# RWKV layer with routed experts: k and v of two token blocks as seven products in place of eight

## Chip, cores, metric

One core of one Trainium2 chip. The metric is device microseconds of one execution: 390.06 us for the kernel before (median of 3 runs, 389.13 to 390.11). Lower is better.

## The reference

An input x of 2048 tokens by 512 channels is layer-normed to xn. Two branches read xn, and their sum is added to x.

- *Attention branch.* `rvk = xn @ W_rvk.T` gives r, v and k. Over the tokens of a sequence runs a recurrence per channel (state o, q, p): `no2 = max(w + o, k)`, `A2 = exp(w + o - no2)`, `B2 = exp(k - no2)`, `q = A2 q + B2`, `p = A2 p + B2 v`, and its output is a quotient of two such sums. The result, times sigmoid(r), goes through `W_out`.
- *Expert branch.* A classifier gives 12 probabilities per token; the top 2 are taken. Eight of the 12 are experts (gate and up 512 to 256, silu, down 256 to 512), four pass xn through with a weight.

All is float32.

## The kernel before

Tokens are cut into four blocks of 512 (`NTB`), channels into four chunks of 128 (`CC`). A *unit* is one (block, chunk).

**Stages.** First each block is loaded, normed (`norm`, L196: VectorE statistics and scaling, ScalarE half of the scaling), transposed on TensorE (`turn_block`, L226, into `xnT`) and put through the classifier. Then routing (L377 to L553), a chain of small VectorE operations with a few matmuls, sorts the tokens into 25 tiles of 128, one expert each. `fill(n)` puts n projection matmuls between those stages, so that TensorE has work: 11 in the loop over blocks, 9, 15 and 7 in the routing, 14 while the first unit of the recurrence starts; 56 of 192.

**Projection** (`project`, L263). A unit takes 12 matmuls: for k, v and r four each, one per 128 input channels, added up in a PSUM bank. The profile shows each matmul as two MATMUL instructions. ScalarE takes the banks to SBUF: copies for k and v (L282), `exp(-r)` for r (L280).

**Recurrence** (`scan`, L286) has four stages per unit, emitted at separate points. First: VectorE copies the state column (L297), scans the running maximum (L301) and forms two exponents (L303, L304). Second: ScalarE's two exponentials (L306, L307). Third: two more scans and the products around them (L313 to L322). Fourth: GpSimd copies part of the last column to the state (L325) for the same chunk's next block, ScalarE the rest; VectorE takes a reciprocal (L327) and writes the product yT (L328). Units run block by block, (0,0), (0,1), ... (3,3), so that a state is next wanted four units later.

**Experts.** `first_half(i)` and `second_half(i)` per tile: GpSimd gathers rows (L561), the DMA transposes 16-bit halves with ScalarE copies around it, `up` (L613) is 4 matmuls, `activate` (L623) is tanh on ScalarE and two VectorE operations, `finish` (L657) is 2 matmuls, a weighting on ScalarE and a GpSimd scatter that adds into `out` (L665). Weights come through SP's queue, `fetch` (L569, 1 MB) and `fetch_down` (L582, 512 KB), each with three buffers.

**Output projection** (`attention`, L727): per 128 tokens 4 matmuls of yT with W_out, a VectorE operation, and for blocks 0 to 2 a GpSimd DMA that adds the rows into `out` (L753). Block 3 reads `out` back, adds and stores.

**Order.** Every engine runs its queue in the order in which the program emits it (`manual_schedule`). The main stretch is written out in a table (L783 to L816): each step has a planned time on TensorE's clock, the steps are sorted by it and emitted. Scan stages come every 19.0 us at offsets 0, 4, 6 and 12 from a start 7 us early; projection and the first two blocks' output projection are spread evenly; expert halves come every `spread`. After the table: output projection of block 2, a branch for surplus tiles that is not taken with these inputs' 25, and block 3.

Of the kernel before, what the change touches and what calls it, by code (L numbers as in the profile page):

```python
# [26 lines left out]
F32 = mybir.dt.float32  # L27
# [8 lines left out]
P = 128  # L36
# [23 lines left out]
def layer(ctx: ExitStack, tc: tile.TileContext, x, w_rvk, w_out, decay, first, cls, ebias, gu, down, out):  # L60
# [6 lines left out]
    keep = pool("keep", 1)  # L67
    xyp = pool("xy", 5)
    ewp = pool("ew", 3)
    gathered = pool("gathered", 2)  # L70
    wk1 = pool("wk1", 1)
    rows = pool("rows", 3)
    basep = pool("base", 4)
    rp = pool("route", 1)
    small = pool("small", 2)
    kvp = pool("kv", 5)
    erp = pool("er", 4)
    wk = pool("wk", 2)
# [12 lines left out]
    def load_x(b):  # L91

        if b < 3:
            t = ewp.tile([P, NJ, C], F32, tag="gw", name=f"x{b}")
        else:
            t = xyp.tile([P, NJ, C], F32, tag="xy", name=f"x{b}")
        for j in range(NJ):
            i = b * NJ + j
            nc.sync.dma_start(t[:, j, :], x[i * P : (i + 1) * P, :])
            xt[i] = t[:, j, :]  # L100
# [57 lines left out]
    for n in range(ET):  # L158
        nc.gpsimd.memset(rank[:, n : n + 1], float(ET - n))

    def iota(shape, pattern, cm, tag, dt, base=0):
        i32 = rp.tile([P, *shape], I32, tag=f"{tag}_i", name=f"{tag}_i")
        nc.gpsimd.iota(i32, pattern=pattern, base=base, channel_multiplier=cm)
        t = const.tile([P, *shape], dt, tag=tag, name=tag)
        nc.gpsimd.tensor_copy(t, i32)
        return t
# [6 lines left out]
    tok_p = iota([1], [[0, 1]], 1, "tok_p", F32)  # L173
    spare = iota([2], [[0, 2]], 1, "spare", F32, T + P)
    one8 = rp.tile([P, E], F32, tag="one8", name="one8")
    nc.gpsimd.memset(one8, 1.0)
# [49 lines left out]
    def turn_block(b):  # L226
        xnT[b] = xyp.tile([P, CC, TB], F32, tag="xy", name=f"xnT{b}")
        for c in range(CC):
            if c % 2 == 0:
                pt = ps_tr.tile([P, TB], F32, tag="tr", name=f"pt{b}_{c}")  # L230
            else:
                pt = ps_gu.tile([P, TB], F32, tag="gu", name=f"pt{b}_{c}")
            for j in range(NJ):
                nc.tensor.transpose(pt[:, j * P : (j + 1) * P], xt[b * NJ + j][:, c * P : (c + 1) * P], ident)
            nc.scalar.copy(xnT[b][:, c, :], pt)
# [26 lines left out]

    def project(b, c):  # L263

        n = f"{b}_{c}"
        for name, m in (("k", 2), ("v", 1), ("r", 0)):
            ps = ps_mm.tile([P, TB], F32, tag="mm", name=f"p{name}{n}")
            for k in range(CC):
                nc.tensor.matmul(  # L269
                    ps,  # L270
                    wrvk_sb[m][:, k, c * P : (c + 1) * P],
                    xnT[b][:, k, :],
                    start=(k == 0),
                    stop=(k == CC - 1),
                )
                if k < CC - 1:
                    yield
            t = (erp if name == "r" else kvp).tile([P, TB], F32, tag=name, name=f"{name}{n}")
            if name == "r":
                nc.scalar.activation(t, ps, AF.Exp, scale=-1.0)  # L280
            else:
                nc.scalar.copy(t, ps)  # L282
            kvr[b, c, name] = t
            yield

    def scan(b, c):  # L286

        n = f"{b}_{c}"
        s = state[c]
        w, cf = wdec[:, c : c + 1], cfac[:, c : c + 1]  # L290
        k = kvr[b, c, "k"]
        if c == 0:
            yT[b] = xyp.tile([P, CC, TB], F32, tag="xy", name=f"yT{b}")


        obv = wk.tile([P, 3, TB + 1], F32, tag="obv", name=f"obv{n}")
        nc.vector.tensor_copy(obv[:, :, 0:1], s[:, 0:3].unsqueeze(2))  # L297
# [10 lines left out]
        yield  # L308

        v = kvr[b, c, "v"]  # L310
        sums = wk1.tile([P, 2, TB], F32, tag="sums", name=f"sums{n}")
# [15 lines left out]
        nc.vector.reciprocal(den, den)  # L327
        nc.vector.tensor_mul(yT[b][:, c, :], num, den)  # L328
        yield

    units = [(b, c) for b in range(NTB) for c in range(CC)]
    LEAD = 4

    def whole(gen):
        for _ in gen:
            pass

    def all_products():
        for u in range(len(units)):
            yield from project(*units[u])  # L340

    products = all_products()

    def fill(n):
        for _ in range(n):
            next(products, None)

# [5 lines left out]
    for b in range(NTB):  # L353
        if b + 1 < NTB:
            norm(b + 1)
        fill(1 if b else 2)
        logits(b)
        fill(1 if b else 3)
        if b + 1 < NTB:
            turn_block(b + 1)  # L360
        add_quarters(b)


    def wide(tag, n=1):
        shape = [P, NT, ET] if n == 1 else [P, n, NT, ET]
        return rp.tile(shape, F32, tag=tag, name=tag)

# [56 lines left out]

    hot8 = rp.tile([P, 2, NT, E], F32, tag="hot8", name="hot8")
    nc.vector.tensor_copy(hot8, hot[:, :, :, :E])
# [18 lines left out]

    over = rp.tile([P, E, NT], F32, tag="over", name="over")
    nc.vector.tensor_tensor(
# [14 lines left out]
    nc.vector.tensor_tensor(pos, pc[:, :NT, :], per_tile(base, E), ALU.add)  # L462
    picked = rp.tile([P, 2, NT, E], F32, tag="picked", name="picked")
    nc.vector.tensor_tensor(
# [15 lines left out]
    def place_tiles():  # L480

        later = rp.tile([P, MAX_TILES, E - 1], F32, tag="later", name="later")
        nc.vector.tensor_tensor(
# [13 lines left out]
    NK = 2 * NT  # L497
    lowhot = xyp.tile([P, NK, P], BF16, tag="xy", name="lowhot")
    pi = ps_o.tile([P, NV, MAX_TILES], F32, tag="o", name="pi")
    fill(15)  # L500
    for m in range(2):
# [6 lines left out]
        )  # L508
        hh = rp.tile([P, NT, MAX_TILES], BF16, tag="hh", name=f"hh{m}")
        nc.vector.tensor_tensor(  # L510
# [4 lines left out]
        )  # L515
        tok = ewp.tile([P, NT, NV, MAX_TILES], BF16, tag="gw", name=f"tok{m}")
        nc.vector.tensor_tensor(
# [20 lines left out]
    nc.vector.tensor_scalar_mul(zw, zw, SCALE)  # L538
    pis = rp.tile([P, NV, MAX_TILES], F32, tag="pis", name="pis")
    nc.vector.tensor_copy(pis, pi)  # L540
# [28 lines left out]
    def fetch(i, which=which_i):  # L569
# [7 lines left out]
        )  # L577
        w = ewp.tile([P, CC, 2 * INTER], F32, tag="gw", name=f"gw{i}")
        nc.sync.dma_start(w, gu[bass.ds(e, 1)].rearrange("o p c n -> p (o c) n"))
        st[i].update(w=w, e=e)  # L580

    def fetch_down(i):  # L582
        d = ewp.tile([P, IC, C], F32, tag="dw", name=f"dw{i}")
        nc.sync.dma_start(d, down[bass.ds(st[i]["e"], 1)].rearrange("o p c n -> p (o c) n"))
        st[i]["d"] = d
# [88 lines left out]
    def first_half(i, n):  # L674

        if i + 2 < n:
            fetch(i + 2)
        if 0 < i < n - 1:
            flip_act(i - 1)
        up(i, (0, 1))  # L680
        if i == n - 1:
            turn_act(i - 1)
        up(i, (2, 3))
        activate(i)
        if i > 1:
            unite_act(i - 2)
        if i + 3 < n:
            gather(i + 3)

    def second_half(i, n):  # L690
# [5 lines left out]
        if i > 1:  # L696
            finish(i - 2)
        if i == n - 1:
            finish(i - 1)
        if 2 <= i + 1 < n:  # L700
            fetch_down(i + 1)

    xrows, orows = {}, {}

    def read_xn(b, js=range(NJ)):
        if b >= NTB - 2:
            t = ewp.tile([P, NJ, C], F32, tag="gw", name=f"xrows{b}")
        for j in js:
# [7 lines left out]
    def read_out(b):  # L716

        t = xyp.tile([P, NJ, C], F32, tag="xy", name=f"orows{b}")
        for j in range(NJ):
# [7 lines left out]
    def attention(b, js=range(NJ)):  # L727

        for j in js:
            i = b * NJ + j  # L730
            if i < (NTB - 2) * NJ - 2:
                po = ps_tr.tile([P, C], F32, tag="tr", name=f"pw{i}")
            elif j >= 2 if i in orows else j % 2 == 1:
                po = ps_mm.tile([P, C], F32, tag="mm", name=f"pw{i}")
# [23 lines left out]
    for i in range(2):  # L758
        fetch(i)
        fetch_down(i)  # L760
    fill(2)
    stages = [scan(*u) for u in units]
    next(stages[0])
    fill(3)
    next(stages[0])
# [10 lines left out]

    UNIT = 19.0
    after = {12: (0, 0), 13: (0, 1), 18: (0, 2), 19: (0, 3), 32: (1, 0), 33: (1, 1), 40: (1, 2), 41: (1, 3)}  # L780
    groups = 3 * (len(units) - LEAD) - 2 + len(after)
    total = groups * 3.43 + TILES * 5.2
    table = []  # L783
# [4 lines left out]
    for u in range(1, len(units)):  # L788
        for at in (0, 4, 6, 12):
            plan((u - 1) * UNIT - 7 + at, stages[u])  # L790
    one = total / groups / CC
    for m in range(groups):
        if m in after:
            b, j = after[m]
            group = attention(b, [j])
            plan(CC * m * one - 16, read_xn, b, [j])

            plan(CC * (m + 2 - j % 2) * one + 1, group)
        else:
            group = products  # L800
        for k in range(CC):
            plan((CC * m + k) * one, group)

# [85 lines left out]
```

## Time and profile before

| | |
|---|---|
| median of 3 runs | 390.06 us |
| profiled execution, its time | 389.55 us |
| its span, first to last instruction | 387.7 us |
| granted TensorE clock, mean | 0.999 |
| pk, pv, pr matmuls (L269) | 3 x 128 instructions, 60.0, 60.9, 60.2 us |
| expert matmuls (L619, L660) | 200 and 100 instructions, 90.1 and 47.1 us |
| output projection (L738) | 128 instructions, 57.5 us |
| reciprocals (L327, VectorE) | 16 x 3.346 us |
| GpSimd scatters (L665) | 25 x 1.661 us |

How to read it: PE is TensorE, DVE VectorE, ACT ScalarE, POOL GpSimd, SP the queue that starts most DMAs; L12 is line 12 of the kernel. A timeline row is start, length, engine, line, operation, output<-inputs, and in brackets the idle time before it and what ended that. The page's cost of a matmul row (595 ns) is longer than the distance from one to the next, because matmuls overlap in the pipeline. TensorE's last work is the output projection of block 3, from 374.0 to 383.7 us.

### The profile page before, as it was taken

To read this page: it belongs to the slowest core of one execution; us is meant where nothing else is said; L and a number is where in the kernel's file an instruction comes from. 1 tells how busy PE (TensorE), PEld (TensorE's weight loads), DVE (VectorE), ACT (ScalarE), POOL (GpSimd) and SP (SyncE) were. 2 spreads that over 40 slices of the span, in tenths; PEclk is the share of its full clock that TensorE was granted. 3 is DMA by queue.
4 is the path that set the end of the run, shared out by engine and by line. 5 is a ranking of instruction groups with operands and counts; after the bars stand their busy time and mean duration, and the time that the engine had idled before them with its cause. 6 is when DMAs were issued, how large, how long until landed. Compare 5 with 4: busy or idle time off the path is not lost. (4 is left out here: it accounts for less than half of the span.)

```text
span 387.7 us, 3521 instructions
## 1 busy us (share of the span) xinstructions
PE 372.0 (96%) x994; PEld 169.7 (44%) x994; DVE 270.6 (70%) x397; ACT 169.8 (44%) x278; POOL 94.4 (24%) x130
## 2 busy tenths in 40 slices
PE   0999999999999999999999999999999999999995
PEld 0465445544444444444444444444444444434442
DVE  5852899799969585858593948685866692949324
ACT  2566211344655554535653554645655354431000
POOL 5000300322232231334222243321322141113400
PEclk9999999999999999999999999999999999999999
DMA  7996945572799797999999897989899999673793
GB/s 285 394 378 251 325 137 193 191 210 63 158 265 304 182 329 194 252 262 230 328 264 266 162 269 213 288 231 230 210 292 274 266 188 236 166 219 46 91 201 115
DMA packets 62884, 88.80 MB, mean 229 GB/s; under 512 B 42192, under 2 KB 42320, under 8 KB 59088
## 3 DMA queue, kind: packets, MB, share of 16 engines
q1 hardware_dynamic: 55328, 67.85, 59.2%
q0 software_dynamic: 7536, 20.71, 24.4%
q8 instruction: 8, 0.13, 0.1%
q14 instruction: 12, 0.10, 0.1%
HBM read 63.78 MB, written 19.40 MB: 215 GB/s over the span
## 5 line engine op out<-in xcount | busy, mean ns | idle before, releaser
L619 PE MATMUL pg<-gw,xgT 128*128 128x512 f32 x200 | 90.1, 592 | 0.0
L665 POOL DMA_INDIRECT out_dram<-yo,to_i x25 | 41.5, 1661 | 156.1 <-ACT yo L664 88.1
L269 PE MATMUL pv<-xnT,wrvk 128*128 128x512 f32 x128 | 60.9, 595 | 1.1 <-DMA wrvk<-in_w_rvk_dram 1.1
L269 PE MATMUL pr<-xnT,wrvk 128*128 128x512 f32 x128 | 60.2, 596 | 0.0
L269 PE MATMUL pk<-xnT,wrvk 128*128 128x512 f32 x128 | 60.0, 600 | 0.0
L619 PEld LDWEIGHTS pg<-gw,xgT 128*128 128x128 f32 x200 | 37.8, 190 | 47.5 <-issue 45.9
L738 PE MATMUL pw<-wout_sb,yT 128*128 128x512 f32 x128 | 57.5, 593 | 0.1
L327 DVE RECIPROCAL den<-den 128x512 f32<-128x512 f32 x16 | 53.5, 3346 | 0.0
L628 DVE SCALAR_TENSOR_TENSOR th<-th,pg 128x256 f32<-128x256 f32 x25 | 10.5, 419 | 56.3 <-ACT th L627 56.3
L660 PE MATMUL po<-dw,actT 128*128 128x512 f32 x100 | 47.1, 593 | 0.8 <-ACT yo L664 0.8
L269 PEld LDWEIGHTS pk<-xnT,wrvk 128*128 128x128 f32 x128 | 24.5, 193 | 31.1 <-issue 30.3
L738 PEld LDWEIGHTS pw<-wout_sb,yT 128*128 128x128 f32 x128 | 24.2, 190 | 30.6 <-issue 30.6
L269 PEld LDWEIGHTS pv<-xnT,wrvk 128*128 128x128 f32 x128 | 23.9, 190 | 31.0 <-issue 28.6
L269 PEld LDWEIGHTS pr<-xnT,wrvk 128*128 128x128 f32 x128 | 23.8, 190 | 29.6 <-issue 28.9
L627 ACT ACTIVATE th<-pg 128x256 f32<-128x256 f32 x25 | 9.6, 383 | 60.4 <-PE pg L619 60.4
L561 POOL DMA_INDIRECT xg<-xs,token_i x25 | 26.1, 1046 | 37.9 <-DVE empty L548 27.4
L313 DVE TENSOR_TENSOR_SCAN sums<-obv,state,a 128x512 f32<-128x512 f32 x16 | 20.5, 1282 | 17.3 <-ACT obv L307 17.3
L660 PEld LDWEIGHTS po<-dw,actT 128*128 128x128 f32 x100 | 18.9, 190 | 25.1 <-issue 22.2
L607 ACT COPY xgT<-xq 128x1024 uint16<-128x1024 uint16 x25 | 29.0, 1160 | 0.0
L599 ACT COPY xp<-xg 128x1024 uint16<-128x1024 uint16 x25 | 26.2, 1046 | 3.5 <-DMA xq<-xp 3.5
L664 ACT ACTIVATE yo<-po,wplace 128x512 f32<-128x512 f32 x25 | 17.2, 687 | 22.3 <-PE po L660 22.3
L315 DVE TENSOR_TENSOR_SCAN sums<-obv,state,a 128x512 f32<-128x512 f32 x16 | 20.6, 1286 | 0.6
(153 smaller groups left out, 353.0 us busy)
## 6 DMA issues: line engine op xcount, KB each, us to landing
gw<-in_gu_dram SPq DMA_DIRECT2D x25, 1024.0 KB, 6.3
dw<-in_down_dram SPq DMA_DIRECT2D x25, 512.0 KB, 4.5
x<-in_x_dram SPq DMA_DIRECT2D x16, 256.0 KB, 6.0
xs<-x SPq DMA_DIRECT2D x16, 256.0 KB, 4.6
wrvk<-in_w_rvk_dram SPq DMA_DIRECT2D x3, 1024.0 KB
xrow<-xs SPq DMA_DIRECT2D x8, 256.0 KB, 4.4
out_dram<-xrow POOLq DMA_DIRECT2D x8, 256.0 KB, 4.0
xrows<-xs SPq DMA_DIRECT2D x8, 256.0 KB, 6.7
```

Of the source, the lines that this page charges most:

```text
L269: nc.tensor.matmul(ps, wrvk_sb[m][:, k, c * P : (c + 1) * P], xnT[b][:, k, :], start=(k == 0), stop=(k == CC - 1),)
L313: nc.vector.tensor_tensor_scan(sq, bs, a2, s[:, 3:4], ALU.add, ALU.mult)
L315: nc.vector.tensor_tensor_scan(sp, bvs, a2, s[:, 4:5], ALU.add, ALU.mult)
L327: nc.vector.reciprocal(den, den)
L561: nc.gpsimd.indirect_dma_start(out=xg, out_offset=None, in_=xs, in_offset=bass.IndirectOffsetOnAxis(ap=token[:, i : i + 1], axis=0),)
L599: nc.scalar.copy(xp, st[i]["xg"].bitcast(U16).rearrange("p (c h) -> p h c", h=2))
L607: nc.scalar.copy(xgT.bitcast(U16).rearrange("p c (t h) -> p c t h", h=2), st[i]["xq"].rearrange("p (h c) t -> p c t h", h=2),)
L619: nc.tensor.matmul(pg, st[i]["xgT"][:, c, :], st[i]["w"][:, c, :], start=(c == 0), stop=(c == CC - 1))
L660: nc.tensor.matmul(po, st[i]["actT"][:, c, :], st[i]["d"][:, c, :], start=(c == 0), stop=(c == IC - 1))
L664: nc.scalar.activation(yo, po, AF.Identity, scale=weight[:, i : i + 1])
L665: nc.gpsimd.indirect_dma_start(out=out, out_offset=bass.IndirectOffsetOnAxis(ap=to[:, i : i + 1], axis=0), in_=yo, in_offset=None, compute ...
L738: nc.tensor.matmul(po, yT[b][:, c, j * P : (j + 1) * P], wout_sb[:, c, :], start=(c == 0), stop=(c == CC - 1),)
```

## The change

Write the stacked weights of k and v as a 2 x 2 matrix of blocks A (rows: k, v; columns: input channels 0 to 255, 256 to 511), and xnT of two token blocks b, b+1 as B (rows: the same channel halves; columns: b, b+1). A B holds k and v of both blocks. Strassen's scheme in Winograd's form needs seven products:

p1 = A11 B11, p2 = A12 B21, p3 = S4 B22, p4 = A22 T4, p5 = S1 T1, p6 = S2 T2, p7 = S3 T3, with S1 = A21 + A22, S2 = S1 - A11, S4 = A12 - S2, S3 = A11 - A21, T1 = B12 - B11, T2 = B22 - T1, T3 = B22 - B12, T4 = B21 - T2. Then k(b) = p1 + p2, k(b+1) = p1 + p6 + p5 + p3, v(b+1) = p1 + p6 + p7 + p5, v(b) = p1 + p6 + p7 + p4.

```diff
+    def sum_weights():
+        nc.gpsimd.tensor_add(s1, a21, a22)
+        nc.gpsimd.tensor_sub(s2, s1, a11)
+        nc.gpsimd.tensor_sub(s4, a12, s2)
+        nc.gpsimd.tensor_sub(s3, a11, a21)          # s3 takes a21's place
+    def sum_x(b, part):
...
+        if part == 0:
+            nc.gpsimd.tensor_sub(t[:, 0], b12, b11)
+            nc.gpsimd.tensor_sub(t[:, 1], b22, t[:, 0])
+        else:
+            nc.gpsimd.tensor_sub(t[:, 0], b22, b12)
+            nc.gpsimd.tensor_sub(t[:, 1], b21, ts[b, 0][:, 1])
...
+    def p1(b, c):
+        ps = bank(ps_mm, "mm", f"px{b}_{c}")
+        yield from two(ps, a11, xnT[b][:, 0:2], c, True)
+        nc.scalar.copy(kvr_tile("v", b, c), ps)
+    def p2(b, c):
+        ps = banks[f"px{b}_{c}"]
+        yield from two(ps, a12, xnT[b][:, 2:4], c, False)
+        nc.scalar.copy(kvr_tile("k", b, c), ps)
+    def p6(b, c):
+        ps = bank(ps_tr, "tr", f"py{b}_{c}")
+        yield from two(ps, s2, ts[b, 0][:, 1], c, True)
+        if (b, c) == (0, 0):
+            yield
+        nc.vector.tensor_add(kvr_tile("k", b + 1, c), kvr[b, c, "v"], ps)
+    def p7(b, c):
+        ps = banks[f"py{b}_{c}"]
+        yield from two(ps, s3, ts[b, 1][:, 0], c, False)
+        nc.vector.tensor_add(kvr_tile("v", b + 1, c), kvr[b, c, "v"], ps)
+    def p5(b, c):
+        ps = bank(ps_mm, "mm", f"pz{b}_{c}") if (b, c) < (0, 2) else bank(ps_tr, "tr", f"pz{b}_{c}")
+        yield from two(ps, s1, ts[b, 0][:, 0], c, True)
+        nc.vector.tensor_add(v, v, ps)              # v(b+1)
+        if (b, c) == (0, CC - 1):
+            sum_x(2, 0)
+            sum_x(2, 1)
+    def p4(b, c):
+        ps = banks[f"py{b}_{c}"]
+        yield from two(ps, a22, ts[b, 1][:, 1], c, False)
+        nc.vector.tensor_add(v, v, ps)              # v(b)
+    def p3(b, c):
+        ps = banks[f"pz{b}_{c}"]
+        yield from two(ps, s4, xnT[b + 1][:, 2:4], c, False)
+        nc.vector.tensor_add(k, k, ps)              # k(b+1)
```

`two` is two matmuls, one per 128 input channels; r keeps its four, in two halves `r(b, c, h)`. The order of the products, cut to its form:

```diff
+        for c in (0, 2):
+            for part in (p1, p2):
+                yield from part(0, c)
+                yield from part(0, c + 1)
+        for c in range(3):
+            for b in (0, 1):
+                yield from r(b, c, 0)
+                yield from r(b, c, 1)
+        for part, c in (
+            (p6, 0), (p6, 1), (p7, 0), (p7, 1), (p4, 0), (p5, 0), (p4, 1), (p3, 0),
+            (p5, 1), (p6, 2), (r, 0), (p3, 1), (p6, 3), (r, 0), (p7, 2), (p7, 3),
+            (p4, 2), (p4, 3), (r, 1), (p5, 2), (r, 1), (p5, 3), (p3, 2),
+        ):
...
+        for c in range(CC):          # second pair: p1 r p6 r p2 p7 r p5 p4 r p3
```

The units run as (0,0), (1,0), (0,1), (1,1), ...: the other block of the same chunk follows at once. The sums of x and of the weights for the first pair are emitted on GpSimd in the loop over blocks, behind `turn_block(1)`. The other lines that bear on time:

```diff
-        obv = wk.tile([P, 3, TB + 1], F32, tag="obv", name=f"obv{n}")
+        obv = wk1.tile([P, 3, TB + 1], F32, tag="obv", name=f"obv{n}")
...
-        nc.vector.tensor_mul(yT[b][:, c, :], num, den)
+        nc.gpsimd.tensor_mul(yT[b][:, c, :], num, den)
...
-        w = ewp.tile([P, CC, 2 * INTER], F32, tag="gw", name=f"gw{i}")
+        w = place.tile([P, CC, 2 * INTER], F32, tag=f"s{7 - i % 2}", name=f"gw{i}")
...
-        if i + 2 < n:
-            fetch(i + 2)
         if 0 < i < n - 1:
             flip_act(i - 1)
         up(i, (0, 1))
...
         activate(i)
+        if i + 2 < n:
+            fetch(i + 2)
...
-    fill(2)
     stages = [scan(*u) for u in units]
     next(stages[0])
-    fill(3)
+    fill(5)
```

Behind these stand: ten shared 1 MB places s0 to s9 (blocks of x, xnT, the sums T, gate weights, yT, rows read back) in place of two pools; gate weights and down weights two buffers each for three; `fetch_down` behind `finish`; a smaller scratch for GpSimd's DMA descriptors (4096). In the table there are 176 products for 192 and 56 done before it as now, so 120 left; a unit comes every 18.84 us; the output projection of blocks 0 and 1 goes in pairs of rows, the first two pairs among the products, (1,0) with (1,1) at `total - 26` and (1,2) with (1,3) at `total - 13`, with both rows' VectorE operations and DMAs behind the pair's eighth matmul; the last products come at `total - 27`. `total` is 260.7 us of planned TensorE work.

## The prediction

> **What bounds the kernel now.** I read the page's busy lines first, then the table of stretches, because the average hides stages with different limits.
>
> ```profile
> span 387.7 us, 3521 instructions
> ...
> PE 372.0 (96%) x994; PEld 169.7 (44%) x994; DVE 270.6 (70%) x397; ACT 169.8 (44%) x278; POOL 94.4 (24%) x130
> ```
> TensorE (PE) is busy for 96% of the span; its work is nearly the time. VectorE (DVE) has 30% left over, on average only:
>
> ```profile
> 39.00:70.00 31.00, 31.00 (x116) 15.42 (x116) 27.84 (x63) 5.47 (x12) 2.95 (x6) 1.00 0.65 234
> 70.00:112.00 42.00, 42.00 (x99) 18.41 (x98) 39.98 (x50) 21.48 (x34) 10.25 (x9) 1.00 0.61 166
> 112.00:356.00 244.00, 243.22 (x570) 107.60 (x569) 169.38 (x203) 121.70 (x197) 69.47 (x58) 1.00 0.93 237
> ```
> Columns: stretch, length, busy PE, PEld, DVE, ACT, POOL. From 70 to 112 VectorE is busy 39.98 of 42 us, as full as TensorE; later 169 of 244. In that early stretch TensorE never waits for it, since projections leave PSUM through ScalarE. Where they meet, in the timelines of PE and DVE:
>
> ```profile
> 67.70 1.54 PE L525 MATMUL pi<-tok,lowhot 128*128 128x200 bf16 x16
> 69.07 1.91 PE L269 MATMUL pv<-xnT,wrvk 128*128 128x512 f32 x4
> ```
> ```profile
> 70.76 0.16 DVE L297 COPY obv<-state 128x3 f32<-128x3 f32 x1
> ...
> 74.19 1.28 DVE L313 TENSOR_TENSOR_SCAN sums<-obv,state,a 128x512 f32<-128x512 f32 x1 [0.70 <-ACT obv L307]
> ...
> 79.33 3.35 DVE L327 RECIPROCAL den<-den 128x512 f32<-128x512 f32 x1
> 82.71 0.69 DVE L328 TENSOR_TENSOR yT<-num,den 128x512 f32<-128x512 f32 x1
> ```
> They give the prices of a recurrence unit: first stage 70.76 to 73.49, i.e. 2.7 us; 0.7 us for ScalarE's exponentials; third stage 74.19 to 79.33, 5.1; reciprocal 82.71 - 79.33 = 3.4; product 0.69.
>
> The timeline of POOL, last and middle part:
>
> ```profile
> 215.23 1.87 POOL L753 DMA_DIRECT2D out_dram<-xrow  x2 [5.46 <-DMA out_dram<-yo,to_i]
> 222.16 1.62 POOL L665 DMA_INDIRECT out_dram<-yo,to_i  x1 [5.06 <-DMA out_dram<-xrow]
> 223.21 0.78 POOL L325 COPY state<-obv 128x3 f32<-128x3 f32 x1
> ```
> ```profile
> 346.12 1.55 POOL L665 DMA_INDIRECT out_dram<-yo,to_i  x1 [8.79 <-ACT yo L664]
> 351.63 1.54 POOL L665 DMA_INDIRECT out_dram<-yo,to_i  x1 [3.97 <-ACT actT L638]
> 357.07 1.55 POOL L665 DMA_INDIRECT out_dram<-yo,to_i  x1 [3.89 <-DMA out_dram<-yo,to_i]
> ```
> GpSimd's writes that add into `out` run one behind another: 5.5 us from a scatter to the next when they queue, 6.9 from a pair of row adds (L753) to the next scatter. All that lies behind them on POOL waits too. Today that is a state copy that is wanted four units later.
>
> **What goes.** k and v take 128 instructions each; seven products for eight leave 224, so 32 fewer. Eight run in 3.43 us (start to start, 39.82 to 43.25 in PE's timeline): 32 x 0.429 = 13.7 us off the engine that sets the end. The one wait for the v weights (L269, 1.1 us at 18.9) goes too: the first 16 products read the k weights alone. ScalarE loses 16 copies of 0.58 us, VectorE 16 products of 0.69 us; both lie beside TensorE and give nothing by themselves. Together **-14.8**.
>
> **What comes, on VectorE.** Each pair of blocks and each channel chunk gets five adds from PSUM: 40 x 0.69 us (row L747, 684 ns, the same shape and an operand in PSUM) = 27.4, less the 11.1 that move away. Unlike the old copies they sit behind the recurrence in VectorE's queue, and TensorE needs them: p7 and p4 accumulate onto the bank that VectorE must have read, p3 onto p5's. I follow both queues in program order from 69.1 on the old clock, products at 0.86.
> - p6(0,0) has run; p6(0,1) ends at 70.8. p7(0,0) needs p6(0,0)'s add, which is issued behind the first stage of the first unit: 73.5 + 0.7 = 74.2. TensorE waits **3.4**.
> - p7(0,0), p7(0,1), p4(0,0) end at 79.4; their last add ends at 80.1, the third stage at 85.3, p5(0,0)'s add at 86.0. TensorE, through p5(0,0) and p4(0,1) at 82.8, wants it for p3(0,0): **3.2**.
> - p3(0,0) ends at 87.7, its add at 88.4; reciprocal 91.8; second unit: 94.5, exponentials 95.2, third stage 100.3; p5(0,1)'s add 101.0. TensorE has p5(0,1), p6(0,2), r and an expert's 3.43, 8.6 in all, to 96.3: **4.7** before p3(0,1).
> - Then VectorE has 15.7 us (two activations of 0.83, reciprocal, first and third stage, four adds) and TensorE 15.5: **0.2**; and reciprocal, activation, add against 3.4 of TensorE: **1.5**.
> Sum **+13.0**. After that a unit's VectorE work is 2.7 + 5.1 + 3.4 + 2.5 adds (1.7) + activations (1.3) + 0.4 = 14.6 of 18.8 planned us, and two other groups (3.4 us and often an expert) lie between an add and its user: I add nothing. From below this step is 0, if each add finds VectorE free; from above 13 and again the 3.4 of one exposed reciprocal for some of the later 24 dependent steps.
>
> **What comes, on GpSimd.** A two-operand sum of 1024 elements has no row. POOL's casts (L165) go from 200 ns for 2 elements to 300 for 128, 0.8 ns an element: 1.0 us is the lower end with one operand. The slowest elementwise row, the reciprocal, gives 6.7 for 1024, the upper end. I take 1.9, POOL's row with its slope doubled, as the nearest; yT's product of 512 is 1.0. The page "GPSIMD Engine Reference" of the Trainium skill (3.1) states 4497 ns for 2048 elements, so about 2.2 us by an estimate from it; the same page (4.1) advises against elementwise work there.
> The first eight sums (15 us) start when block 0's stores have landed (about 27) and end before TensorE wants them (about 62): no cost if they disturb nobody. The four for the second pair fall at planned 46, with 18 to spare.
>
> **The tail.** yT's product and the state copy of a unit are now in POOL's queue, and the next unit (the other block, same channels) needs that state at once. In the middle the copy came before the next first stage even in today's trace (223.21 + 0.78 against 224.32, the tightest). At the end the order is: row adds (1,2) and (1,3), scatters 22 and 23, then state copy and product of unit (2,3), scatter 24, the last product. Let S be the start of block 2's output projection. TensorE ends the row pair 5.5 us before S, VectorE's two ops end at S-4.4; scatter 22 at S+2.5, 23 at S+8.0, copy S+9.7, product done S+10.7. TensorE wants it for its fourth matmul, S+2.6: **8.1**. The last unit starts at S+9.7 and takes 2.7 + 0.7 + 5.1 + 3.4; VectorE then clears the bank for block 3's first row at S+22.5, TensorE could use it at S+21.9: 0.6. Sum **+8.7**; 0 if POOL is through in time, 6 more if the DMAs land as late as in the middle (8.3 for 5.5).
>
> The moved loads (gate weights behind `up`, two buffers for three) land in 6.3 us and are wanted two rounds of 9.9 later: 0; without that cover each costs what it is late.
>
> **Sum.** 387.7 - 14.8 + 13.0 + 8.7 = 394.6 span; the profiled run's time was 389.55, 1.85 above its span: 396.5. That run lies 0.5 under the median of 390.06: **397.0**, slower.
>
> **Rivals.**
> - *The sums hide* (faster): TensorE keeps its rhythm. Neither wait 375.2; the tail's alone 383.9; the early one alone 388.2. For: VectorE has 75 idle us from 112 on, and the waits above rest on a hand count of two queues. Against: 39.98 of 42. It decides by whether VectorE reaches p6(0,0)'s add before 71. Price 380.
> - *The port* (slower still). Rows first: POOL's state copy is 0.19 us alone, but 1.14 at 76.22, ending at 77.36, with VectorE's scan of 76.10 to 77.38:
>
> ```profile
> 76.22 1.14 POOL L325 COPY state<-obv 128x3 f32<-128x3 f32 x1 [3.34 <-DVE obv L314]
> ```
>   GpSimd waits for VectorE; whether VectorE waits for GpSimd no row shows, POOL's ops being so short. If so, block 3's normalisation (VectorE 29.2 to 31.7, wanted by TensorE at 32.1) ends with the eight sums, 27 + 15.2 = 42.2 and not 31.7: up to 10.5, **407.5**. "SBUF — State Buffer" (SBUF: two separate sides) calls the shared pair an exclusive lock held for a whole instruction, by either side; by that rule this is the sum, and with its 2.2 us an add 2.4 more.
> - *Smaller waits* (same): both a third shorter, 390.
> - *Not what it says*: were the products not fewer, 411; the diff's count (7 x 2 + 2 x 4 matmuls for 24 a chunk) excludes it.
>
> **How the numbers follow.** Forecast (391.2 to 405) 0.44; port (405 to 415) 0.22; hidden (374 to 388.9) 0.28; same 0.06. The range 380 to 412 leaves out about half of the hidden case's lower end (0.1) and the end of the port's (0.08). A measurement can tell about 0.3%, 388.9 to 391.2. Faster 0.28, same 0.06, slower 0.66.
>
> **What would show it.** Right: PE idle before p7 and p3 between 70 and 125, released by VectorE; PE idle behind POOL's yT at the end; PE busy 358. Wrong: PE at 96% or more with DVE near 80% (then 380); or PE idle at 32 to 45 with VectorE's tiny ops stretched (the port). If POOL's sums run 2.5 us or more, or p6 waits for them at 62, the sum misses that.

## The result, and the profile after

The changed kernel takes **419.06 us** (median of 4 runs, 418.54 to 423.64) against 389.66 for the kernel before in the same session (4 runs): ratio 1.0781, 95% interval 1.0703 to 1.0859. The profiled execution took 419.39, its span is 417.5, so 29.8 were added to 387.7. In several runs below a few executions lie over 1.5% above the fastest of the same kernel; times (medians), ratios and intervals leave these out, and where such an execution or its profile is used, the text gives its time.

The page of the changed kernel, busy times, TensorE's slices and its granted clock:

```profile
PE 374.7 (90%) x962; PEld 169.8 (41%) x962; DVE 302.6 (72%) x421; ACT 161.2 (39%) x262; POOL 148.5 (36%) x158
...
PE   0995999697599999999999999999999999953996
...
PEclk9997799988889999999999999999999999969799
```

The 32 matmuls less are there (994 to 962), yet TensorE is busy 2.7 us longer. 372.0 - 13.7 would be 358.3, so 16.4 us are work at a lower clock, and idle time grew from 15.7 to 42.8, by 27.1: 16.4 + 27.1 - 13.7 = 29.8. Both are in the same three places: slices 4 and 5, 8 to 12, and 36 to 38. TensorE's waits, in us in total, number, longest:

```profile
PE pt L245 <- DVE x L232: 15.2, 3, 10.1
PE pz L321 <- DVE v L368: 7.9, 2, 4.8
PE pw L895 <- POOL yT L493: 6.3, 1, 6.3
PE po L817 <- DVE xrow L907: 4.3, 1, 4.3
PE py L321 <- issue: 3.2, 1, 3.2
```

The 10.1 is the wait for the first load (9.4 before). By landmarks in both timelines the loss is: **prologue** +8.9 (first projection matmul after the router's last at 77.94, was 69.07), **early stretch** to the first tile's down product (133.36, was 108.69) +15.8 although 1.7 of products are gone, **middle** to block 2's output projection (376.05, was 355.66) -4.3 where 12.0 were saved, **end** +9.4. The first two landmarks in the changed kernel, and the second in the kernel before:

```profile
77.94 1.91 PE L321 MATMUL py<-t,sw 128*128 128x512 f32 x4
...
133.36 1.88 PE L817 MATMUL po<-dw,actT 128*128 128x512 f32 x4
```
```profile
108.69 1.88 PE L660 MATMUL po<-dw,actT 128*128 128x512 f32 x4
```

*Prologue.* VectorE, block 3's normalisation, in the kernel before and in the changed kernel, then GpSimd's sums beside it:

```profile
30.41 0.16 DVE L215 TENSOR_TENSOR rstd<-r,sq 128x4 f32<-128x4 f32 x1
30.61 0.16 DVE L216 SCALAR_TENSOR_TENSOR shift<-mv,rstd 128x4 f32<-128x4 f32 x1
30.69 1.00 DVE L221 TENSOR_SCALAR x<-x,mv,rstd 128x512 f32<-128x512 f32 x2
```
```profile
29.57 0.17 DVE L225 TENSOR_SCALAR sq<-sq 128x4 f32<-128x4 f32 x1
29.77 2.28 DVE L226 TENSOR_TENSOR rstd<-r,sq 128x4 f32<-128x4 f32 x1
32.08 0.16 DVE L227 SCALAR_TENSOR_TENSOR shift<-mv,rstd 128x4 f32<-128x4 f32 x1
32.16 5.07 DVE L232 TENSOR_SCALAR x<-x,mv,rstd 128x512 f32<-128x512 f32 x2
```
```profile
29.67 2.35 POOL L310 TENSOR_TENSOR t<-xnT,xnT 128x1024 f32<-128x1024 f32 x1 [24.20 <-DVE sq L224]
32.11 2.35 POOL L311 TENSOR_TENSOR t<-xnT,t 128x1024 f32<-128x1024 f32 x1
34.43 2.52 POOL L313 TENSOR_TENSOR t<-xnT 128x1024 f32<-128x1024 f32 x1
```

An operation on four elements a partition takes 2.28 us (0.16 before) and ends with GpSimd's first sum (32.02); the two scalings, 1.00 before, take 5.07 and end 0.3 us behind its third sum (36.95). TensorE, in windows of 2 us (busy times of PE, PEld, DVE, ACT, POOL, then the granted clock):

```profile
32.00:34.00 2.00, 0.00 (x0) 0.00 (x0) 1.97 (x3) 1.72 (x3) 1.92 (x2) 1.00 0.59 225
...
36.00:38.00 2.00, 0.71 (x4) 0.72 (x5) 1.23 (x1) 0.00 (x0) 2.00 (x2) 0.50 0.49 186
...
44.00:46.00 2.00, 2.00 (x9) 0.34 (x10) 0.00 (x0) 0.61 (x2) 1.92 (x2) 0.50 0.00 0
46.00:48.00 2.00, 2.00 (x11) 1.49 (x12) 0.07 (x1) 1.82 (x2) 2.00 (x2) 0.94 0.02 4
48.00:50.00 2.00, 2.00 (x6) 0.81 (x6) 1.39 (x5) 0.93 (x3) 2.00 (x4) 1.00 0.00 0
```

It waits 5.1 us and then works at half clock to 46: wait and clock together are the 8.9.

*Early stretch.* The three waits in TensorE's timeline:

```profile
83.06 7.08 PE L321 MATMUL py<-t,wrvk 128*128 128x512 f32 x12 [3.22 <-issue]
...
96.66 3.04 PE L321 MATMUL pz<-xnT,sw 128*128 128x512 f32 x4 [3.08 <-DVE v L368]
...
113.73 3.78 PE L321 MATMUL pz<-xnT,sw 128*128 128x512 f32 x4 [4.81 <-DVE v L368]
```

The forecast had 3.4, 3.2 and 4.7. The first, put down to "issue", ends with L354, the first addition from PSUM (the profile of `no_first_sums` names it); the other two end with p5's, which stands behind the third stage of the recurrence. With each the clock falls to 0.50 (84 to 87, 97 to 101, 111 to 118).

*End.* GpSimd's queue:

```profile
368.90 1.77 POOL L910 DMA_DIRECT2D out_dram<-xrow  x2 [7.54 <-DVE xrow L907]
376.22 1.62 POOL L822 DMA_INDIRECT out_dram<-yo,to_i  x1 [5.55 <-DMA out_dram<-xrow]
382.02 1.55 POOL L822 DMA_INDIRECT out_dram<-yo,to_i  x1 [4.18 <-DMA out_dram<-yo,to_i]
383.04 0.73 POOL L490 COPY state<-obv 128x3 f32<-128x3 f32 x1
383.19 1.80 POOL L493 TENSOR_TENSOR yT<-num,den 128x512 f32<-128x512 f32 x1
```

State copy and yT stand behind two scatters, each behind the addition before it, as forecast; TensorE waits 6.27 for yT, VectorE 11.28 for the state.

### The profile page after: what moved, and what is told of

The parts are those of the page before. It is cut to its first block, busy times and chain, and to the rows that moved or that the text cites. A ratio compares the mean times of both kernels' runs of the same rounds, so it can differ in the third digit from the quotient of the medians.

```text
span 417.5 us, 3511 instructions
## 1 busy us (share of the span) xinstructions
PE 374.7 (90%) x962; PEld 169.8 (41%) x962; DVE 302.6 (72%) x421; ACT 161.2 (39%) x262; POOL 148.5 (36%) x158
## 5 line engine op out<-in xcount | busy, mean ns | idle before, releaser
L895 PE MATMUL pw<-wout_sb,yT 128*128 128x512 f32 x128 | 59.8, 618 | 6.4 <-POOL yT L493 6.3
L817 PE MATMUL po<-dw,actT 128*128 128x512 f32 x100 | 49.0, 614 | 5.0 <-DVE xrow L907 4.3
L493 POOL TENSOR_TENSOR yT<-num,den 128x512 f32<-128x512 f32 x16 | 24.9, 1555 | 55.1 <-DVE den L492 45.2
L718 POOL DMA_INDIRECT xg<-xs,token_i x25 | 29.9, 1196 | 33.8 <-DVE empty L705 27.5
L895 PEld LDWEIGHTS pw<-wout_sb,yT 128*128 128x128 f32 x128 | 25.2, 199 | 39.6 <-issue 32.2
L321 PE MATMUL py<-t,wrvk 128*128 128x512 f32 x64 | 32.0, 623 | 3.2 <-issue 3.2
L321 PE MATMUL px<-xnT,wrvk 128*128 128x512 f32 x64 | 33.6, 636 | 0.0
L764 ACT COPY xgT<-xq 128x1024 uint16<-128x1024 uint16 x25 | 28.9, 1156 | 10.8 <-DMA xq<-xp 10.6
L756 ACT COPY xp<-xg 128x1024 uint16<-128x1024 uint16 x25 | 26.1, 1043 | 11.3 <-DMA xg<-xs,token_i 8.0
L478 DVE TENSOR_TENSOR_SCAN sums<-obv,state,a 128x512 f32<-128x512 f32 x16 | 22.5, 1406 | 5.6 <-ACT obv L471 5.3
L321 PE MATMUL pz<-xnT,sw 128*128 128x512 f32 x32 | 18.8, 694 | 7.9 <-DVE v L368 7.9
L245 PE MATMUL pt<-ident,x 128*128 128x128 f32 x64 | 11.7, 346 | 15.3 <-DVE x L232 15.2
```

The lines of the kernel that those rows point to most:

```text
L321: nc.tensor.matmul(ps, a[:, k, c * P : (c + 1) * P], x[:, k], start=(start and k == 0), stop=(k == 1), skip_group_check=True,)
L478: nc.vector.tensor_tensor_scan(sq, bs, a2, s[:, 3:4], ALU.add, ALU.mult)
L493: nc.gpsimd.tensor_mul(yT[b][:, c, :], num, den)
L718: nc.gpsimd.indirect_dma_start(out=xg, out_offset=None, in_=xs, in_offset=bass.IndirectOffsetOnAxis(ap=token[:, i : i + 1], axis=0),)
L756: nc.scalar.copy(xp, st[i]["xg"].bitcast(U16).rearrange("p (c h) -> p h c", h=2))
L764: nc.scalar.copy(xgT.bitcast(U16).rearrange("p c (t h) -> p c t h", h=2), st[i]["xq"].rearrange("p (h c) t -> p c t h", h=2),)
```

## The experiments

Theory: the port of the forecast's rival, VectorE's queue and GpSimd's queue each hold TensorE, and the clock enlarges every wait. Rivals: VectorE is simply too full; order and buffers cost it, not the scheme.

**no_first_sums**

```diff
-            sum_x(0, 0)
-            sum_x(0, 1)
-            sum_weights()
+            ts[0, 0] = ts[0, 1] = xnT[0].rearrange("p (h c) t -> p h c t", h=2)
```
(and `s1, s2, s4 = a22, a11, a12`)

> The changed kernel without the eight sums of the first pair on GpSimd (its products read the weights and the normalised blocks as they stand; the sums' work is left out). Port theory: VectorE's normalisation of block 3 is no longer held by GpSimd's 2.35 us sums, so TensorE's 5.1 us of waiting at 32 to 39 us and the half clock from 36 to 46 us go; the first p6(0,1) comes at about 69 us in place of 77.9, and the time falls by about 9, to 410 (408 to 413). If VectorE is simply too full, or if the half clock has nothing to do with the wait, the time stays within 2 of 419. The waits at 80 to 114 and the tail stay in either case.

409.94, ratio 1.0496 (1.0433 to 1.0559): 9.1 less. The first projection matmul after the router comes at 67.28, the clock is 1.00 from 30 to 50:

```profile
67.28 1.91 PE L321 MATMUL py<-xnT,wrvk 128*128 128x512 f32 x4
```

The prologue's loss is the sums.

**port_alone** (the kernel before with)

```diff
+            for n in (0, 2, 0, 2):
+                nc.gpsimd.tensor_sub(dead, x1[:, n : n + 2], x0[:, n : n + 2])
+            for n in (0, 2, 0, 2):
+                nc.gpsimd.tensor_add(dead, wv_t[:, n : n + 2], wk_t[:, n : n + 2])
```

> The kernel before with nothing of the change but eight dead GpSimd sums of two operands, 1024 elements each, at the place where the change puts its sums (results go nowhere; for room the DMA scratch is 4096 as in the change). Port theory: VectorE's small operations of block 3's normalisation wait behind the sums, TensorE waits about 5 us at 32 to 39 us, then runs at half clock for some 8 us: about 9 slower, 398.5 (396 to 401). If GpSimd's sums block nobody, the time stays at 390 (389 to 391). If the wait costs only itself, without the clock, it is about 395.

401.81, ratio 1.0297 (1.024 to 1.0353): 11.8 slower, above the expected 396 to 401; the sums start earlier (22.23) and meet the normalisation of two blocks. VectorE:

```profile
24.64 0.16 DVE L213 TENSOR_TENSOR sq<-sq,ve 128x4 f32<-128x4 f32 x1
24.84 2.20 DVE L214 TENSOR_SCALAR sq<-sq 128x4 f32<-128x4 f32 x1
27.08 0.16 DVE L215 TENSOR_TENSOR rstd<-r,sq 128x4 f32<-128x4 f32 x1
27.27 2.19 DVE L216 SCALAR_TENSOR_TENSOR shift<-mv,rstd 128x4 f32<-128x4 f32 x1
```

One operation in two is held for about a whole sum. Nothing reads those sums, so the hold is not a dependency of the program: the two engines share something.

**pieces**

```diff
-        nc.gpsimd.tensor_add(s1, a21, a22)
+        for k in range(2):
+            for h in range(0, TB, 256):
+                nc.gpsimd.tensor_add(s1[:, k, h : h + 256], a21[:, k, h : h + 256], a22[:, k, h : h + 256])
```
(so for all sums, in four pieces each)

> The changed kernel with each of the twelve sums cut into four GpSimd instructions of 256 elements. Port theory with an alternation by instruction: a small VectorE operation waits for one piece (about 0.6 us) and no longer for a whole sum (2.35 us), so block 3's normalisation loses about 2 us in place of 7, and most of TensorE's 5.1 us and of the half clock behind it goes: 412 (410 to 415). If GpSimd holds the port for as long as it has work queued, the size of a piece changes nothing and the time stays at 418 to 421.

410.43 and 412.04 in two executions, 422.34 and 423.29 in two others. In the profile of the 410.43 the held operations are short:

```profile
28.93 0.16 DVE L226 TENSOR_TENSOR rstd<-r,sq 128x4 f32<-128x4 f32 x1
29.12 0.71 DVE L227 SCALAR_TENSOR_TENSOR shift<-mv,rstd 128x4 f32<-128x4 f32 x1
29.75 1.90 DVE L232 TENSOR_SCALAR x<-x,mv,rstd 128x512 f32<-128x512 f32 x2
```

So the hold goes by the piece, as expected, in that execution. `all_copies` below cuts the sums in the same way; the profile of its 403.88 execution (the others took 392.46, 396.39 and 403.83) has this row:

```profile
39.64 12.43 DVE L548 TENSOR_TENSOR route<-route,sm 128x192 f32<-128x192 f32 x1
```

It took 0.62 in the profile of `pieces`. 52.07 is where GpSimd's last piece has ended (51.86): there one operation was held over piece after piece, and TensorE waited 11.6 for the router. So pieces made the hold shorter in one profile and not in the other. What made the two longer executions of `pieces` isn't shown: they have no profile.

**late**

```diff
-        if b == 0:
+        if b == 2:
+            nc.gpsimd.tensor_copy(sw[:, 0, 0, 0:2], shift[:, 14:16])
+            sum_weights()
             sum_x(0, 0)
             sum_x(0, 1)
-            sum_weights()
```

> The changed kernel with the first pair's eight sums held back until block 3's normalisation has its shift (a small copy ahead of them on GpSimd reads it). If the port loss is one of place, the wait and the half clock of the prologue go and the router's operations, behind which TensorE has products queued, bear the sums: 410 (408 to 413). If every short VectorE operation beside a sum is held, the router's chain of short operations loses as much as the normalisation did, TensorE waits for it at 60 to 80 us, and the time is 416 to 423.

415.15, ratio 1.0683 (1.0618 to 1.0748): neither 410 nor no gain. The hold moves to the router:

```profile
40.46 2.33 DVE L546 TENSOR_TENSOR route<-route,bias_sb 128x192 f32<-128x192 f32 x1
42.83 0.35 DVE L552 TENSOR_REDUCE top<-route 128x16 f32<-128x192 f32 x1
43.22 2.00 DVE L554 TENSOR_TENSOR route<-route,top 128x192 f32<-128x192 f32 x1
```

TensorE waits 6.8 for the router's `hotb`, in place of the 5.1 for the normalisation; 4 us are gained, not the 9.

**copies** (so at all five)

```diff
-        nc.vector.tensor_add(k, k, ps)
+        nc.scalar.copy(k, ps)
```

> The changed kernel with the five additions from PSUM on VectorE replaced by plain ScalarE copies (the sums of the products are left out). Queue theory: TensorE no longer stands behind VectorE at 80 to 114 us (3.2, 3.1 and 4.8 us) nor at half clock after it; stage two shrinks from 55.4 to about 39 us, the time falls by about 17 to 402 (399 to 406). If the loss there came from the new order of the products or from buffers, the waits stay under other names and the time is 415 to 419. If ScalarE takes VectorE's place as the engine waited for, 410 to 416.

406.49, ratio 1.0414 (1.0357 to 1.0471): 12.6 less, of the 17 expected. The two waits that are left are behind ScalarE. The longer one's copy stands behind a copy for a tile, idle for 3.26 us until a transpose lands (91.09); the shorter one's starts when a VectorE operation of the recurrence ends (L468, at 81.92):

```profile
PE pz L321 <- ACT v L368: 3.0, 1, 3.0
PE py L321 <- ACT k L354: 1.6, 1, 1.6
```

**adds_first**

```diff
+        if m == 1:
+            fill(1)
         for j in range(NT):
...
-    fill(5)
+    fill(4)
     next(stages[0])
-    fill(4)
+    fill(7)
     next(stages[0])
...
-    fill(5)
+    fill(2)
...
-        plan(m * one, group)
+        plan(m * one - (6 if m < 4 else 0), group)
```

> The changed kernel with the first additions from PSUM moved ahead of the recurrences on VectorE's queue: k(1,0) before the end of the router, p5(0,0) and p4(0,1) before the third part of unit (0,0), p5(0,1) and p6(0,2) before that of unit (1,0); nothing is taken out. Queue theory: the waits of 3.1 and 4.8 us before p3(0,0) and p3(0,1) go, that of 3.2 before p7(0,0) shrinks, and with them most of the half clock at 84 to 118 us; stage two goes from 55.4 to about 43 us and the time to 408 (404 to 413). If VectorE is simply full there, the wait only moves to a later product or exponential, and the time stays at 416 to 421.

415.43, ratio 1.0669 (1.0651 to 1.0687): 3.6 less, between the two answers and nearer to "VectorE is full there". `all_fixes` has the same order, and its profile shows where the waits went:

```profile
PE pg L783 <- ACT xgT L771: 6.1, 3, 3.0
PE pz L326 <- DVE v L373: 3.2, 1, 3.2
PE py L326 <- DVE k L359: 2.5, 1, 2.5
```

From 11.1 before the products to 5.7, and 6.1 before experts' products (4.8 of it in this stretch). VectorE works 24.5 of 25 us between 90 and 115. Order alone doesn't heal that stretch; work has to leave VectorE.

**tail_off_pool**

```diff
-            nc.gpsimd.tensor_copy(s[:, 0:3].unsqueeze(2), obv[:, :, TB : TB + 1])
+            nc.scalar.copy(s[:, 0:3].unsqueeze(2), obv[:, :, TB : TB + 1])
-        nc.gpsimd.tensor_mul(yT[b][:, c, :], num, den)
+        nc.vector.tensor_mul(yT[b][:, c, :], num, den)
```

> The changed kernel with the last product of each unit (yT) back on VectorE and the copy of the state on ScalarE, so that GpSimd has neither behind its scatters and row pairs. Queue theory of the tail: TensorE's 6.3 us behind GpSimd's yT at 379 to 385 and the half clock after it go, VectorE's 11.3 us behind the state copy too: 7 to 9 faster, 411 (409 to 414). If the tail's loss is the late row load on SyncE's queue instead, at most 3 faster, 416 to 419. If VectorE is too full to take the sixteen products, the early waits grow by some us and the time stays at 417 to 421.

415.73, ratio 1.0591 (1.0487 to 1.0695): 3.3 less, where 7 to 9 were expected. TensorE's wait for yT is gone, but the end is now the chain of additions into the output: 20.6 us from 376.9, of scatters one behind another, 6.4 for the rows to come back, then the last sums.

**base4**

```diff
-    basep = pool("base", 3)
+    basep = pool("base", 4)
-    nc = bacc.Bacc("TRN2", target_bir_lowering=False, num_devices=1, dynamic_dma_scratch_size=4096)
+    nc = bacc.Bacc("TRN2", target_bir_lowering=False, num_devices=1, dynamic_dma_scratch_size=2048)
```

> The changed kernel with four row buffers again in place of three (room by a DMA scratch of 2048). SyncE theory: the row load of 357.27 no longer waits 11.4 us for a row's write, the transpose of the activations behind it runs some 6 us earlier, TensorE's waits of 4.3 and 0.7 us before the last scattered tiles and the clock after them go: 413 (410 to 415). If the chain of writes into the output on GpSimd's queue sets that stretch, the wait keeps its size under another name and the time stays at 417 to 420.

421.48, ratio 1.08 (1.0758 to 1.0842): no gain. The load no longer waits, TensorE's waits of 4.3 and 0.7 are gone, and it waits under other names:

```profile
PE pw L895 <- POOL yT L493: 10.0, 1, 10.0
...
PE po L817 <- DMA dw<-in_down_dram: 3.8, 1, 3.8
```

So the late load does make the 4.3, but it doesn't set the time: GpSimd's chain (10.0 in place of 6.3) and the weights with two buffers (3.8) stand right behind it. (The smaller scratch went with it; what that does alone wasn't tried.)

**tail_both** (tail_off_pool, and)

```diff
-    for n, at in ((2, end + 1), (3, end + 14)):
-        plan(at - 16, read_pair, n)
+    for n, at in ((2, end + 1), (3, end + 23)):
+        plan(at - (16 if n == 2 else 13), read_pair, n)
```

> The changed kernel with yT on VectorE and the state copy on ScalarE, and besides with the last pair of rows of block 1 (its load, its product, its addition into the output) put behind the last scattered tile. Theory: once GpSimd's yT is out of the way, the end is set by the additions into the output, which go one behind the other (a scatter waits about 5.6 us for the one before, 7 for a row pair); without the pair in front of the last three scatters they come 7 us earlier, and the late row load no longer stands before the last transposes: 408 (404 to 412). If the time was lost to earlier waits and to the clock alone, it stays where the first of the two remedies left it, 414 to 417.

408.42, ratio 1.0476 (1.0428 to 1.0523): 10.6 less than the changed kernel, 7.3 less than tail_off_pool. In the profiles block 3's rows are read back by 397.74, in tail_off_pool by 405.06: with the pair behind the last scatter the chain is shorter. The end's loss was two things in one queue.

**all_fixes** (the diffs of pieces, adds_first and tail_both together)

> The changed kernel with all remedies: sums in pieces of 256, first additions ahead of the recurrences, yT and state copy off GpSimd, last row pair behind the last scatter. If the causes are separate, their gains add: about 8, 3.5 and 10 off 419 give 398 (394 to 404), still above the kernel before, for VectorE's additions in the early stretch remain. If they share one cause (VectorE full), each remedy only moves the wait and the time stays above 406.

405.56, ratio 1.0392 (1.0354 to 1.043): 13.5 of the 21.5 that the parts would sum to. So the remedies overlap; where is read from the waits above, not tested.

**second_pair and plain_alt**

```diff
+        for b in (0, 1):
+            for c in range(CC):
+                yield from project(b, c)
-        rest = iter([r(b, 3, h) for b in (0, 1) for h in (0, 1)])
...
```
(Strassen's products for blocks 2 and 3 alone, sums during block 1, tail as in tail_both; plain_alt: `project` there too)

> Strassen's scheme only for blocks 2 and 3: blocks 0 and 1 have their k and v by the plain products, in the order of the kernel before, and their recurrences one block after the other; the sums of weights and of blocks 2 and 3 run on GpSimd during block 1; yT, state copy and last row pair as in tail_both. Half the saving remains (16 products less, 0.86 less 0.43 us of filling each: 6.9 us). Theory: in the middle stretch TensorE has work queued, so VectorE's additions and GpSimd's sums cost nothing there; the early stretch is that of the kernel before: 390 - 7 + 0 to 6 at the end for the recurrences that alternate = 386 (382 to 391). If GpSimd's sums or VectorE's additions cost time in the middle as well, 392 to 400.

> As second_pair, but without any Strassen product or sum: all k and v by plain products, the changed kernel's buffers, its alternating recurrence for blocks 2 and 3, yT, state copy and last row pair as in tail_both. It tells what the alternation and the buffers cost by themselves: if nothing, 390 (388 to 391); if the two last recurrences together delay the last rows, 393 to 399. Its distance to second_pair is what the scheme itself brings where TensorE has work queued: about 7.

395.66, ratio 1.0142 (1.0102 to 1.0182), and 401.38, ratio 1.0283 (1.0235 to 1.033), the second above both of its expected ranges. Two answers. In the middle the scheme does bring most of its saving, 5.7 of 6.9 (some 2 us either way, for `plain_alt` spreads from 397.91 to 403.78); in the profiles TensorE has its last 80 instructions of output projection left at 353.28 and 358.77, 5.5 apart. But order and buffers alone, without one product of the scheme, cost 11.3, which the forecast had at 0 (with the end of `tail_both`, and the alternation for blocks 2 and 3 alone). TensorE's waits in plain_alt beside those at the start:

```profile
PE po L822 <- DMA dw<-in_down_dram: 2.9, 1, 2.9
PE pr L411 <- ACT k L424: 2.6, 1, 2.6
...
PE po L822 <- ACT actT L813: 1.0, 1, 1.0
```

**second_pair2 and plain_alt2**

```diff
+    fill(2)
     stages = [scan(*u) for u in units]
     next(stages[0])
-    fill(5)
+    fill(3)
...
+        if i == TILES - 1:
+            d = place.tile([P, IC, C], F32, tag="s1", name=f"dw{i}")
...
+        if i == n - 2:
+            fetch_down(n - 1)
```

> second_pair with two waits taken away that its profile shows and that the kernel before hasn't: two products are issued ahead of the first recurrence again (TensorE waited 2.4 us for a ScalarE copy behind that recurrence's exponentials, and ran slower after it), and the last tile's weights go to a place that is free early (TensorE waited 3.0 us for them). If the order and the buffers made these waits, 395.7 - 2.4 - about 2 of clock - 3 = 388 (385 to 391). If the alternating recurrence sets the end whatever stands before it, 393 to 396.

> plain_alt (no Strassen product) with the same two waits taken away: 401.4 - 2.6 - about 2 - 2.9 = 394 (391 to 397) if they are what the order and the buffers cost; 398 to 402 if the alternation costs it. The distance to second_pair2 is again what the scheme brings for one pair: 5 to 7.

394.16, ratio 1.0106 (1.008 to 1.0132), and 397.81 (397.29 to 403.01), ratio 1.0239 (1.0188 to 1.029). Only 1.5 and 3.6 less: the wait for the weights is gone, that for ScalarE's copy (2.6) is not, so `fill` was not its cause. The copy stands behind a ScalarE copy for tile 1, which waits for a transpose. The distance is 3.7 by the medians and 5.2 by the ratios: the scheme's gain for one pair again, no better known than before.

**all_copies** (the diffs of pieces, tail_both and copies, and the last tile's weights of second_pair2)

> The changed kernel with all that the runs pointed to at once, and VectorE's additions of the products' sums left out (ScalarE copies in their place): sums in pieces of 256, yT and state copy off GpSimd, last row pair and last tile's weights as in second_pair2. If the three causes are all there is, copies' 406.5 less 8 for the port, 10 for the tail and 3 for the weights gives 386 (382 to 391): the saved work shows at last. If something else holds the time, it stays above 395.

392.46 and 396.39, ratio 1.0114 (1.0059 to 1.017), and 403.83 and 403.88 in two others: not 386, and nearer to "something else holds the time". Port, additions and tail are most of the loss, not all.

**second_pair3** (second_pair2, each sum one unit later, and)

```diff
-            nc.scalar.copy(s[:, 0:3].unsqueeze(2), obv[:, :, TB : TB + 1])
+            nc.vector.tensor_copy(s[:, 0:3].unsqueeze(2), obv[:, :, TB : TB + 1])
...
-    flip(1)
     fill(5)
+    flip(1)
...
-    for n, at in ((2, end + 1), (3, end + 23)):
+    for n, at in ((2, end - 16), (3, end + 23)):
```

> second_pair2 with what its profile shows late: the state copy on VectorE (0.16 us in the same queue), the second transposed tile issued behind the k and v copies on ScalarE (TensorE waited 2.6 and 1.7 us for them at 81 to 93), GpSimd's sums one unit later, beside no early recurrence, and the other row pair of block 1 a tile earlier, since the end is now set by the chain of additions into the output (last scatter at 364.3, rows back at 385.2, while TensorE had ended at 384.8). If queue order is what is left, 394.2 - 4 to 6 = 389 (386 to 391), level with the kernel before or just under it. If the alternating recurrence itself sets the end, 392 to 395.

**388.88** against 389.56, ratio 0.9978 (0.9955 to 1.0001), 11 executions against 17: level with the kernel before. The waits of 2.6 and 1.7 are gone. TensorE's last output projections here, then in the kernel before:

```profile
345.99 25.05 PE L914 MATMUL pw<-wout_sb,yT 128*128 128x512 f32 x58
```
```profile
353.08 20.76 PE L738 MATMUL pw<-wout_sb,yT 128*128 128x512 f32 x48
```

22 follow in each, so 80 are left at 345.99 and 70 at 353.08. With 70 left this kernel stands at 350.28, 2.8 ahead, and it ends 2.8 ahead, at 380.88 for 383.69. The other 4.1 of the 6.9 are in waits that it has more of: 3.0 for `actT` before the experts' last products (0.8 for `yo` before), 2.4 for the v weights (1.1), 0.5 for `xgT`. Of the 2.8, most goes to the chain of additions (in the chain that ended last, start and length):

```profile
358.89 11.89 DMA out_dram<-yo,to_i
...
372.72 7.46 DMA orows<-out_dram
```

The last scatter at 358.89 and what is behind it in GpSimd's queue hold the read of block 3's rows to 372.72, and these are back at 380.18, when TensorE is almost through: behind TensorE's end the kernel before has 4.0 left, this one 6.5. That leaves 0.3 of the span (387.4 for 387.7).

## Why the prediction was wrong, point by point

The direction, slower, was right; the time is 22.1 above the forecast's 397.0.

- *What goes, -14.8*: right in matmuls (32 fewer, 13.7 at full clock), and the wait of 1.1 for the v weights is gone; `second_pair` against its twin got 5.7 of 6.9 where TensorE had work queued.
- *VectorE's queue, +13.0*: right in mechanism and size. 3.22 + 3.08 + 4.81 = 11.1 us of waiting for 11.3; the two small ones didn't come. With the clock the stretch lost 17.5.
- *GpSimd's sums, "no cost if they disturb nobody"*: **failed**, and it is the first term. They disturbed: 8.9. It stood as a rival, *the port*, with 10.5 and a chance of 0.22, and that rival's row, GpSimd held by VectorE, was the sign. A sum takes 2.35 and not 1.9, but in this profile VectorE gets in between two sums, so the hold didn't last to the end of all eight as the rival had it: 5.1 of waiting, and the rest is clock.
- **The clock has no term**: the second failure, and the larger. Each wait was priced at itself; the runs show part of it again as lower clock, 16.4 in all (part of the losses by stretch). Idle time alone, 27.1 for the net 20.6 forecast (13.0 + 8.7 - 1.1), would have given 397.0 + 6.5 = 403.5.
- *The tail, +8.7*: right in its queue, 6.27 for 8.1 of wait, 9.4 with the clock. Taking GpSimd's part out of it brought 3.3 (`tail_off_pool`), the row pair in the same chain 7.3 more (`tail_both`): the forecast had the pair in the order, but not as a second bound.
- *"I add nothing" after the early stretch, moved loads 0*: **failed**, by 7.7. Waits of 4.3, 0.7 and 1.0 and the clock behind them make up most of that, out of 12.0 saved. The 4.3 is a path that the forecast didn't follow: a transpose stands behind the row load on SyncE's queue (345.48 to 357.61), ScalarE's tanh behind that, a recurrence's third stage on VectorE behind that (from 362.73), and behind this the operation on `xrow` (367.86) that TensorE waits for. Without the load's wait (`base4`) it is gone, but nothing is gained, for the next waits stand behind it. `plain_alt` puts order and buffers at 11.3 without the scheme; the weights' load with two buffers and ScalarE's queue are parts of it (`second_pair2`, `second_pair3`). How the rest divides stays open.

The changed kernel's time is thus the forecast's early waits and its tail, the rival's port, 7.7 in the middle, and a clock that nobody priced.

## What to carry to other kernels

On an engine that is 96% busy, fewer matmuls are worth only as much as the other engines' queues let through: follow each new operation in its own queue, and don't price a wait of 3 us or more on TensorE at itself: here it cost 1.5 to 1.7 times that (8.9 for 5.1, 17.5 for 11.1, 9.4 for 6.3). Elementwise work on GpSimd is not free beside VectorE, least of all beside a chain of tiny operations. Put the saving where TensorE has work queued, and check what ends last after it.

## What the runs showed of the hardware

- *Clock.* Every wait of 3 us and more in the changed kernel, but for the first (10.1, before any work of TensorE), came with a stretch at 0.50: 3 to 7 us of it, and 10 us in the prologue, where transposes follow. 2.4 us in `second_pair` lowered the mean of 70 to 90 us to 0.91; 2.6 us in `second_pair2` left it at 1.00. The Trainium skill, "TensorE: Matmul & The Clock Gate" (Part 1: The HAM clock gate), has half rate after an idle window of about 3.4 us and full rate after a busy one. The 4.81 agrees with that; 3.08 and 3.22 are a little shorter than the window, and the 2.4 of `second_pair` and the prologue's 10 us don't agree.
- *Port.* GpSimd's sums hold VectorE's additions and scalings, not its reductions (0.35 us beside a sum in `late`). Mostly the hold ends with the running sum; once it lasted 12.43 us over many. "SBUF — State Buffer" (SBUF: two separate sides) says that the lock is kept "for the whole instruction", which agrees with the 2.28 and not with the 12.43. Which operation meets a sum differs by execution: in the profile of the 422.0 execution of `adds_first` (others 415.03 to 415.53) four small VectorE operations are held 2.2 us each at 29 to 39, and TensorE waits 11.1 for the normalisation, not 5.1.
- *Times by execution.* `plain_alt`, without sums, spreads by 5.9 (397.91 to 403.78), at clocks of 0.994 to 0.985, the kernel before by 4.1 over all sessions (388.82 to 392.94); what does that stays open.
